# Overlapping image strips in HBM: stored once by line, and cut into strips by the loads

## The chip, the cores and the metric

The kernel runs on one NeuronCore of a Trainium2 chip. Its time is the device time of one execution in microseconds; less is better. Three runs of the kernel before gave a median of 8800.12 us (8797.13 to 8805.94). One further execution was taken by the hardware profiler, and the profile below is of that one.

## What is computed

The input `x` is (4, 64, 256, 256): 4 images, 64 channels, 256 lines of 256 columns, all in float32. Two layers follow one another. The first is a transformer block on images: a layernorm, an attention over channels with a local branch, a residual, a second layernorm and a gated feed-forward pass with depthwise convolutions and a filter of 8 x 8 patches in the frequency domain. The second is a linear attention over rows, one over columns, and an ordinary feed-forward pass. The change touches the gated feed-forward pass of the first layer:

```python
def _mffn(x, in_w, dw3, dw5, out_w, fW):
    t = _conv1x1(x, in_w)                      # 64 -> 256 channels
    x1, x2 = (t[:, :192], t[:, 192:])
    d1 = _dwconv(x1, dw3)                      # 3 x 3, each channel by itself
    x_gate, x1_2 = (d1[:, :128], d1[:, 128:])
    x2 = _dwconv(x2, dw5)                      # 5 x 5, each channel by itself
    y = gelu(x_gate) * concatenate([x1_2, x2], axis=1)
    y = _conv1x1(y, out_w)
    ...                                        # patch filter
```

`t` are the 256 inner channels that the title of the change speaks of; they travel through HBM between two stages of the kernel.

## The kernel before

The program runs in stages, one after another: A (first layernorm, projections, attention statistics), a short rest of the local branch, C1, C2, C3 (output product, patch filter, row attention) and D (column attention and feed-forward pass). Each stage reads what the one before it left in HBM. C1 and C2 matter here.

**C1** walks over 32 blocks of 8 image lines, with two pairs of images in each. For a block it builds the residual stream `xm` (matmuls L775 and L779, DVE L785), transposes and normalizes it (L796, L797, layernorm), turns it back (L810, L812) and multiplies by the feed-forward input weights. That last part is `hidden(s, hf)`: `hf` 0 and 1 stand for the two halves of the 256 inner channels, 128 partitions each. For every two lines, four matmuls (L824, one per image) are copied into a tile `tb` (ACT L830 and DVE L828 in turn) and stored to the HBM tensors `td[0]` or `td[1]` by DMAs that POOL issues: one for `hf` 0 (L842), and two for `hf` 1 (L839, L840), since there the two halves of the column phases change places. A column is 4 t + f, with f its phase and t from 0 to 63; a *line* of one channel and one phase holds 4 images x 64 values of t, which is 1 KB.

**C2** does the depthwise convolutions as banded matmuls, one channel pair (one channel of `td[0]`, one of `td[1]`) per group, 128 groups. The partitions of the operand `t0` or `t1` are the pairs (f, line in strip): 4 phases x 32 lines. An image of 256 lines is covered by NI = 9 strips of 32 lines which begin R0 = 28 lines apart, so neighbouring strips share four lines. The band matrices `w` contract over phases and lines at once (`full`, L882, 128 x 128), and two 64 x 64 parts per tile add what comes from the neighbouring t (`part`, L889). ACT L914 takes the gelu, DVE L915 the product into `y`, and POOL L916 stores `y` to `yd`.

`load(g)` of C2 issues three DMAs on SP's queue: `w` (L872, 192 KB) and `t0`, `t1` (L876, 1152 KB each), into tiles with three buffers. It is called two groups ahead, so the loads of group g + 2 stand in the program before the work of group g and wait for the end of group g - 1, whose buffers they take. The framework that places waits does so from what each instruction reads and writes; nothing else orders the two stages, and the first load of C2 waits for the last store of C1.

In the kernel before, `td` is laid out by strip: `[128 channels, 9 strips, 4 phases, 32 lines, 256]`. A line that lies in two strips is stored twice, by a second DMA from the same `tb`. A strip is then one block of 128 lines of 1 KB, and the load of `t` one DMA for all 128 partitions.

Elsewhere in the program there are loads that reach only some partitions: `xs` of stage A in halves of 64 (L511), `L` of the local branch in quarters of 32 (L445), and `gp` in pieces of 32 and 64 partitions (L592 to L600 in stage A, L745 to L749 in C1).

Of the kernel before, what the change touches and what calls it, by code (L numbers as in the profile page):

```python
# [9 lines left out]
F32 = mybir.dt.float32  # L10
# [4 lines left out]
C, H, W = 64, 256, 256  # L15
# [234 lines left out]
def kernel(ctx: ExitStack, tc: tile.TileContext, x, packs, fd, out, off):  # L250
    nc = tc.nc
    B = x.shape[0]
    V, S, T, G, SY = nc.vector, nc.scalar, nc.tensor, nc.gpsimd, nc.sync
# [3 lines left out]
    dram = ctx.enter_context(tc.tile_pool(name="dram", bufs=1, space=bass.MemoryType.DRAM))  # L257

    def mm():
        return ps.tile([128, 512], F32, tag="mm", name="mm")  # L260
# [22 lines left out]


    NI, R0 = 9, 28
    td = [dram.tile([128, NI, 4, 32, B * W // 4], F32, name=f"td{v}") for v in (0, 1)]
    yd = dram.tile([128, 4, 32, NI, B * W // 4], F32, name="yd")


# [37 lines left out]
    p = sp1.enter_context(tc.tile_pool(name="pst", bufs=2))  # L327
# [386 lines left out]
    def stage_c1():  # L714
        NS = H // 8
        with ExitStack() as cs:
            p = cs.enter_context(tc.tile_pool(name="pc", bufs=2))
# [3 lines left out]
            t = mm()  # L721
# [6 lines left out]
            t = mm()  # L728
# [88 lines left out]
            def hidden(s, hf):  # L817

                for y in range(4):
                    tb = p.tile([128, 8, B, W // 4], F32, name="tb", bufs=5)  # L820
                    for b in range(B):
                        q = slice(b % 2 * 64, b % 2 * 64 + 64)
                        t = mm()
                        T.matmul(t, inT[q, hf * 128:(hf + 1) * 128],  # L824
                                 xls[b // 2, s][q, :, 2 * y:2 * y + 2].rearrange("p f y t -> p f (y t)"), start=True, stop=True)
                        o, i_ = tb[:, :, b, :], t.rearrange("p (f t) -> p f t", f=8)
                        if b % 2:
                            V.tensor_copy(o, i_)  # L828
                        else:
                            S.copy(o, i_)  # L830
                    y0 = 8 * s + 2 * y
                    tf = tb.rearrange("p (f y) b t -> p f (y b t)", f=4)
                    for i in range(NI):
                        r = y0 - R0 * i
                        if 0 <= r < 32:
                            dst = td[hf][:, i, :, r:r + 2].rearrange("g f r e -> g f (r e)")

                            if hf:
                                G.dma_start(dst[:, 2:4], tf[:, 0:2])  # L839
                                G.dma_start(dst[:, 0:2], tf[:, 2:4])  # L840
                            else:
                                G.dma_start(dst, tf)  # L842
                    yield

            def after(*gens):
# [10 lines left out]
            for n in range(len(seq) + 3):  # L856
                if n + 1 < len(seq):
                    load(*seq[n + 1])
                _steps(after(back(*seq[n - 2]) if 1 < n < len(seq) + 2 else None, hidden((n - 3) // 2, (n - 3) % 2) if n > 2 else None),
                       front(*seq[n]) if n < len(seq) else None)  # L860
# [4 lines left out]
    def stage_c2():  # L865
        with ExitStack() as cs:
            p = cs.enter_context(tc.tile_pool(name="pe", bufs=2))
            NW = 192

            def load(g):  # L870
                w = p.tile([128, 2 * NW], F32, name="w", bufs=3)
                SY.dma_start(w, fd[:, 2 * NW * g:2 * NW * (g + 1)])  # L872
                xs = []
                for v in (0, 1):
                    t = p.tile([128, NI * B, W // 4], F32, tag=f"t{v}", name=f"t{v}", bufs=3)
                    SY.dma_start(t.rearrange("p (n b) t -> p n (b t)", b=B), td[v][g].rearrange("n f r e -> (f r) n e"))  # L876
                    xs.append(t)
                ld[g] = w, xs

            def full(t, w, x_, c):  # L880
                n = (c.stop - c.start) * 64
                T.matmul(t[:, :n], w[:, 0:128], x_[:, c, :], start=True, stop=False, skip_group_check=True)  # L882

            def part(t, w, x_, c, dt, turned):

                n = (c.stop - c.start) * 64
                o, i_, po = (slice(0, 63), slice(1, 64), 64) if dt > 0 else (slice(1, 64), slice(0, 63), 0)
                q = 64 - po if not turned else po
                T.matmul(t[po:po + 64, :n].rearrange("p (n c) -> p n c", c=64)[:, :, o], w[q:q + 64, 128:192],  # L889
                         x_[q:q + 64, c, i_], start=False, stop=True, skip_group_check=True)  # L890

            ld = {}
            load(0)
            load(1)
            for g in range(128):
                if g + 2 < 128:
                    load(g + 2)
                w, xs = ld.pop(g)
                y = p.tile([128, NI * B, W // 4], F32, name="y", bufs=3)
                ws = [w[:, v * NW:(v + 1) * NW] for v in (0, 1)]  # L900
                for i in range(0, NI, 4):
                    cs_ = [slice(k * B, min(k + 2, NI) * B) for k in range(i, min(i + 4, NI), 2)]
                    ts = [[mm() for c in cs_] for v in (0, 1)]
                    for v in (0, 1):
                        for t, c in zip(ts[v], cs_):
                            full(t, ws[v], xs[v], c)
                    for k, c in enumerate(cs_):
                        for dt in (1, -1):
                            for v in (0, 1):
                                part(ts[v][k], ws[v], xs[v], c, dt, v)  # L910
                    for k, c in enumerate(cs_):
                        n = (c.stop - c.start) * 64
                        ge = p.tile([128, 512], F32, name="ge", bufs=4)
                        S.activation(ge[:, :n], ts[0][k][:, :n], AF.Gelu)  # L914
                        V.tensor_tensor(y[:, c, :].rearrange("p n c -> p (n c)"), ge[:, :n], ts[1][k][:, :n], ALU.mult)  # L915
                G.dma_start(yd[g].rearrange("f r n e -> (f r) (n e)"), y.rearrange("p n t -> p (n t)"))  # L916
# [496 lines left out]
```

## Time and profile before

| | before |
|---|---|
| three runs: median (lowest to highest) | 8800.12 us (8797.13 to 8805.94) |
| the profiled execution | 8803.6 us |
| its span on the core | 8801.8 us |
| granted TensorE clock, mean | 0.969 |
| HBM read, written | 967.65 MB, 788.53 MB |
| queue q1 (SP's loads), share of 16 engines over the span | 39.0% |
| queue q0 (POOL's stores), share of 16 engines over the span | 28.0% |
| `t<-td` loads, L876 | 256 of 1152 KB, median 9.9 us from issue to landing |
| `td<-tb` stores, L842 | 144 of 1024 KB, median 15.6 us |
| `td<-tb` stores, L839 and L840 | 288 of 512 KB, median 13.9 us |

The profile names an instruction by its line, its engine and the tiles it writes and reads (`t<-td`). PE is the engine of the matmuls, PEld its weight loads, DVE the vector engine, ACT the scalar engine, POOL and SP the two that issue DMAs here. All DMAs run on the same 16 DMA engines, whichever queue they come from. A share of 16 engines is the time that the packets of a queue took, divided by 16 times the length of the stretch. In the rows of 40 slices a digit is the busy share in tenths of one fortieth of the span (220 us). A row of waits reads: who waited, for whom, us in total, times, longest.

### The profile page before, as it was taken

Reading aid. Unit: us, or ns where it says so; the run is one execution under the profiler, and the core shown is the slowest. Engines: PE = TensorE matmul, PEld = TensorE weight load, DVE = VectorE, ACT = ScalarE, POOL = GpSimd, SP = SyncE. Lnnn points to the kernel's source line nnn. Section 1 sums busy time; section 2 is a strip of 40 time slices with the busy share of each in tenths; the row PEclk is TensorE's granted clock in tenths of the full one; section 3 lists DMA queues with packets and bytes.
Section 4 is the critical chain, followed back from the end, with each engine's and each line's share of the span. In section 5 each row is a group of like instructions: output and inputs, shape, how many; then the busy total and the mean of one; then the engine's idle time right before and its main releaser. Section 6 shows DMA issues by size and latency. Waiting matters only on the chain. (4 is left out here: it accounts for less than half of the span.)

```text
span 8801.8 us, 143151 instructions
## 1 busy us (share of the span) xinstructions
PE 8178.1 (93%) x57518; PEld 4216.6 (48%) x57518; DVE 5927.4 (67%) x8506; ACT 4601.7 (52%) x7779; POOL 1205.2 (14%) x1828
## 2 busy tenths in 40 slices
PE   8999999699999998999999999999997999999998
PEld 6777777344444443333333344444443444444443
DVE  7766666377777774222222288888886888888886
ACT  4455455455555553222222266666663777777776
POOL 1111111212222221000000011111110010101011
PEclk9999999699999999999999999999997999999999
DMA  7777777799999998888888755555552232323232
GB/s 161 161 188 187 182 182 180 193 347 388 396 391 388 386 387 320 298 296 298 296 297 298 273 184 172 173 168 167 169 158 63 59 77 58 77 58 77 58 77 39
DMA packets 1258502, 1832.48 MB, mean 208 GB/s; under 512 B 335600, under 2 KB 1040112, under 8 KB 1196656
## 3 DMA queue, kind: packets, MB, share of 16 engines
q1 hardware_dynamic: 1053296, 1034.63, 39.0%
q0 software_dynamic: 204544, 788.69, 28.0%
q8 instruction: 456, 7.47, 0.3%
q14 instruction: 206, 1.69, 0.1%
HBM read 967.65 MB, written 788.53 MB: 200 GB/s over the span
## 5 line engine op out<-in xcount | busy, mean ns | idle before, releaser
L915 DVE TENSOR_TENSOR y<-ge,mm 128x512 f32<-128x512 f32 (+1 forms) x640 | 406.3, 635 | 1212.8 <-ACT ge L914 1212.8
L882 PE MATMUL mm<-t,w 128*128 128x512 f32 (+1 forms) x2560 | 1094.1, 566 | 18.8 <-DMA t<-td 18.8
L914 ACT ACTIVATE ge<-mm 128x512 f32<-128x512 f32 (+1 forms) x640 | 354.9, 555 | 1253.5 <-PE mm L889 1253.5
L775 PE MATMUL mm<-gp,wc 128*64 128x510 f32 (+1 forms) x3072 | 702.7, 596 | 90.8 <-DVE xm L785 51.4
L620 PEld LDWEIGHTS mm<-wqk,gp 128*128 128x128 f32 x6144 | 728.7, 197 | 99.2 <-issue 61.5
L882 PEld LDWEIGHTS mm<-t,w 128*128 128x128 f32 x2560 | 455.4, 190 | 647.5 <-issue 437.0
L620 PE MATMUL mm<-wqk,gp 128*128 128x128 f32 x6144 | 762.3, 282 | 1.1 <-POOL gp L589 0.9
L1341 PE MATMUL mm<-xfT,w 64*128 64x512 f32 x2048 | 620.9, 642 | 51.1 <-ACT hg L1343 26.8
L1343 ACT ACTIVATE hg<-mm,b 128x512 f32<-128x512 f32 x1024 | 634.1, 688 | 53.2 <-PE mm L1341 51.5
L830 ACT COPY tb<-mm 128x512 f32<-128x512 f32 x512 | 300.7, 588 | 632.4 <-PE mm L824 632.1
L889 PE MATMUL mm<-t,w 64*64 64x504 f32 (+1 forms) x5120 | 575.6, 555 | 0.0
L824 PE MATMUL mm<-xl,pack_c 64*128 64x512 f32 x2048 | 513.5, 601 | 8.1 <-ACT xl L812 4.7
L1358 PE MATMUL mm<-hg,pack_d 128*64 128x512 f32 x2048 | 505.8, 615 | 0.0
L775 PEld LDWEIGHTS mm<-gp,wc 128*64 128x64 f32 x3072 | 277.8, 137 | 470.5 <-issue 333.3
L316 ACT ACTIVATE ln_sq<-xn 128x1024 f32<-128x1024 f32 x256 | 274.3, 1072 | 365.4 <-DVE xn L314 365.3
L1365 POOL DMA_DIRECT2D out_dram<-st x128 | 209.1, 1638 | 1756.3 <-DVE fe L695 1543.6
L318 DVE TENSOR_REDUCE ln_v<-ln_sq 128x16 f32<-128x1024 f32 x256 | 312.0, 1219 | 186.0 <-ACT ln_sq L316 186.0
L970 PE MATMUL mm<-ya,pack_e 128*64 128x512 f32 x1024 | 381.2, 616 | 11.2 <-DMA ya<-yd 11.2
L828 DVE COPY tb<-mm 128x512 f32<-128x512 f32 x512 | 345.0, 685 | 24.0 <-PE mm L824 18.5
L1359 DVE TENSOR_SCALAR st<-mm,pack_d 128x512 f32<-128x512 f32 x256 | 281.1, 1098 | 117.9 <-PE mm L1358 117.6
L1341 PEld LDWEIGHTS mm<-xfT,w 64*128 64x128 f32 x2048 | 225.1, 192 | 276.1 <-issue 125.7
L1185 ACT ACTIVATE ln_sq<-xc 128x1024 f32<-128x1024 f32 x256 | 273.0, 1067 | 132.1 <-DVE xc L1183 132.1
(458 smaller groups left out, 15283.8 us busy)
## 6 DMA issues: line engine op xcount, KB each, us to landing
t<-td SPq DMA_DIRECT2D x256, 1152.0 KB, 9.9
td<-tb POOLq DMA_DIRECT2D x144, 1024.0 KB, 15.6
td<-tb POOLq DMA_DIRECT2D x288, 512.0 KB, 13.9
yd<-y POOLq DMA_DIRECT2D x128, 1152.0 KB, 10.1
ya<-yd SPq DMA_DIRECT2D x192, 512.0 KB, 5.7
xs<-in_x_dram SPq DMA_DIRECT2D x128, 512.0 KB, 6.8
projd<-pj POOLq DMA_DIRECT2D x256, 256.0 KB, 6.0
gp<-projd SPq DMA_DIRECT2D x128, 512.0 KB, 9.5
```

Of the source, the lines that this page charges most:

```text
L620: T.matmul(qp[:, k * 128:(k + 1) * 128], gp[:, 2 * i + k // 2, at + dx:at + dx + 128], wqk[:, dx, :], start=(dx == 0), stop=(dx == 2))
L775: T.matmul(tv[i * 64:(i + 1) * 64, :, o], wc[2 * pr + i][:, dx, :], gps[i][:, 2 * r:2 * r + 2, i_], start=(dx == 1), stop=False, skip_grou ...
L824: T.matmul(t, inT[q, hf * 128:(hf + 1) * 128], xls[b // 2, s][q, :, 2 * y:2 * y + 2].rearrange("p f y t -> p f (y t)"), start=True, stop=True)
L828: V.tensor_copy(o, i_)
L882: T.matmul(t[:, :n], w[:, 0:128], x_[:, c, :], start=True, stop=False, skip_group_check=True)
L889: T.matmul(t[po:po + 64, :n].rearrange("p (n c) -> p n c", c=64)[:, :, o], w[q:q + 64, 128:192], x_[q:q + 64, c, i_], start=False, stop=Tr ...
L914: S.activation(ge[:, :n], ts[0][k][:, :n], AF.Gelu)
L915: V.tensor_tensor(y[:, c, :].rearrange("p n c -> p (n c)"), ge[:, :n], ts[1][k][:, :n], ALU.mult)
L970: T.matmul(t[b * 64:(b + 1) * 64, :], owT, ya[:, :, 2 * r:2 * r + 2, b * 64:(b + 1) * 64].rearrange("p f y t -> p y f t"), start=True, sto ...
L1341: T.matmul(t, w1[rh * 64:(rh + 1) * 64, k * 128:(k + 1) * 128], xT[rh * 64:(rh + 1) * 64], start=True, stop=True)
L1343: S.activation(g, t, AF.Gelu, bias=b1[:, k:k + 1])
L1358: T.matmul(y[rh * 64:(rh + 1) * 64, :], w2[:, k, :], hg[k * 2 + rh], start=False, stop=(k == 1), skip_group_check=True)
```

## The change

`td` is laid out by image line: `[128 channels, 4 phases, 260 lines, 256]`, of which lines 0 to 255 are written and read. Each pair of lines is stored once; the loop over strips in `hidden` goes, and with it the second store of shared lines. The strips are cut by the loads: the load of `t0` or `t1` becomes four DMAs, one for each phase f. Each goes to 32 partitions, and reads 32 lines (step 1 KB) of 9 strips (step R0 lines, 28 KB), 1 KB from each. Lines shared by two strips are read twice, as before. The tiles in SBUF, the matmuls and everything else stay.

```diff
-    td = [dram.tile([128, NI, 4, 32, B * W // 4], F32, name=f"td{v}") for v in (0, 1)]
+    td = [dram.tile([128, 4, H + 4, B * W // 4], F32, name=f"td{v}") for v in (0, 1)]
...
                     tf = tb.rearrange("p (f y) b t -> p f (y b t)", f=4)
-                    for i in range(NI):
-                        r = y0 - R0 * i
-                        if 0 <= r < 32:
-                            dst = td[hf][:, i, :, r:r + 2].rearrange("g f r e -> g f (r e)")
-
-                            if hf:
-                                G.dma_start(dst[:, 2:4], tf[:, 0:2])
-                                G.dma_start(dst[:, 0:2], tf[:, 2:4])
-                            else:
-                                G.dma_start(dst, tf)
+                    dst = td[hf][:, :, y0:y0 + 2].rearrange("g f r e -> g f (r e)")
+
+                    if hf:
+                        G.dma_start(dst[:, 2:4], tf[:, 0:2])
+                        G.dma_start(dst[:, 0:2], tf[:, 2:4])
+                    else:
+                        G.dma_start(dst, tf)
...
                     t = p.tile([128, NI * B, W // 4], F32, tag=f"t{v}", name=f"t{v}", bufs=3)
-                    SY.dma_start(t.rearrange("p (n b) t -> p n (b t)", b=B), td[v][g].rearrange("n f r e -> (f r) n e"))
+                    for f in range(4):
+
+                        src = td[v][g, f]
+                        win = bass.AP(tensor=src.tensor, offset=src.offset, ap=[[B * W // 4, 32], [R0 * B * W // 4, NI], [1, B * W // 4]])
+                        SY.dma_start(t[f * 32:f * 32 + 32].rearrange("p (n b) t -> p n (b t)", b=B), win)
                     xs.append(t)
```

## The prediction

> **What bounds the kernel now.** I read the busy line and the 40 slices first, then asked the trace for the stretches of the two stages that the change touches: C1 (about 1720 to 3410 us, it writes `td`) and C2 (3420 to 5042 us, it reads `td`).
>
> ```profile
> PE 8178.1 (93%) x57518; PEld 4216.6 (48%) x57518; DVE 5927.4 (67%) x8506; ACT 4601.7 (52%) x7779; POOL 1205.2 (14%) x1828
> ...
> PE   8999999699999998999999999999997999999998
> ...
> DMA  7777777799999998888888755555552232323232
> GB/s 161 161 188 187 182 182 180 193 347 388 396 391 388 386 387 320 298 296 298 296 297 298 273 184 172 173 168 167 169 158 63 59 77 58 77 58 77 58 77 39
> ```
>
> PE is busy nearly throughout, and two stages also have DMA engines close to full: slices 9 to 15 (C1, some 390 GB/s) and 16 to 22 (C2, some 297 GB/s). In such stages one must ask which of the two sets the pace. For C2, the timeline of PE over one channel group:
>
> ```profile
> 4007.99 3.70 PE L882 MATMUL mm<-t,w 128*128 128x512 f32 x8
> ...
> 4020.02 0.66 PE L889 MATMUL mm<-t,w 64*64 64x252 f32 x8
> 4020.60 0.70 PE L882 MATMUL mm<-t,w 128*128 128x512 f32 x1
> ```
>
> (start, duration, instruction.) One group takes 4020.60 - 4007.99 = 12.61 us, and PE has no gap in it. PE's waits over the stage and the DMA queues of 3500 to 5000 us:
>
> ```profile
> PE mm L882 <- DMA t<-td: 18.8, 1, 18.8
> ```
>
> ```profile
> q1 hardware_dynamic: 294810, 303.84, 64.4%
> q0 software_dynamic: 17138, 140.40, 22.1%
> ```
>
> PE waits for a load once, at the stage's start. The 16 DMA engines are used 64.4 + 22.1 = 86.5%: PE sets the pace, but only 1.7 us of each 12.61 us are free on the DMA engines. That is the whole cover.
>
> For C1 the trace holds an experiment of its own. Some steps store a pair of lines twice (strips overlap), some once. Three equal stretches of two steps each, columns: stretch, length, busy us (count) of PE, PEld, DVE, ACT, POOL, clock, DMA share, GB/s:
>
> ```profile
> 2109.69:2160.99 51.30, 48.67 (x240) 23.59 (x240) 40.83 (x57) 27.82 (x49) 9.80 (x15) 1.00 1.02 375
> 2160.99:2212.53 51.54, 48.92 (x240) 23.65 (x240) 40.74 (x57) 27.81 (x49) 12.88 (x19) 1.00 1.02 395
> 2316.57:2367.90 51.33, 48.68 (x241) 23.60 (x241) 40.66 (x57) 27.86 (x49) 11.45 (x17) 1.00 1.02 393
> ```
>
> The second has four POOL instructions, all DMA issues, more than the first (19 against 15) and is 0.24 us longer; the third has two more and is 0.03 us longer. So the second copies cost C1 nearly nothing, although its DMA engines read as full.
>
> **The change, part by part.**
>
> *Stores (C1).* 144 stores of 1 MB per array become 128: 16 of L842's and 32 of L839/L840's go, 2 x 16 x 1.05 = 33.6 MB. POOL is saved 48 x 0.7 us (0.72 us each in the stretches above) on an engine busy 14%: nothing. PE's gain by the rows above is 0.03 us for two extra issues to 0.24 us for four: 48 issues give 1 to 3 us. PE's waits between 1850 and 3300 us give an upper end for relief: 3.3 us for `gp`. I take -3. The last stores (lines 248 to 255) were stored once already, so the drain that C2's first load waits for stays. The store's pieces stay 2 KB; only its address steps change (1152 to 1040 KB from channel to channel, 32 to 260 KB from f to f). No row shows such a change alone; between 1% of C1's 1630 us lost and as much won (16 us, my estimate: PE covers the rest, as in the three stretches) I take nothing.
>
> *SP's issues (C2).* Two `t` loads per group become eight. L876's median issue is 0.422 us, so SP spends 6 x 0.42 = 2.5 us more per group, beside its waits of 11 us per group for PE (1333.0 us in 123 waits). Hidden. Behind them in SP's queue stand only the next group's loads.
>
> *PE's waits (C2).* The first matmul of a group now depends on nine loads, not three. The trace has semaphore instructions of 51 ns at L882, two per group; six more are 0.3 us per group, 39 us over 128 groups if nothing hides them, 0 if PE waits for data anyway. I take 0; the 39 belongs to the rival below.
>
> *Size and number of packets.* Bytes (2 x 1.18 MB per group) and pieces (1 KB) are unchanged; the new pattern steps 28 KB from strip to strip where the old one stepped 128 KB. No row shows such a step alone: between nothing and the loss that I leave to the slow rival.
>
> *32 partitions per load.* This is the term that matters. Each quarter load writes 32 partitions: f = 0, 1 the lower 64, f = 2, 3 the upper 64. `t` now takes, per group, q1's 64.4% of 1500 us over 119 groups = 8.12 us of all 16 engines, of which `w` has 0.20 of 2.56 MB = 0.62 us, leaving 7.5 us for 2.36 MB: 315 GB/s. How fast are loads that reach only part of the partitions? Stage A loads `xs` as 64 partitions in one half, in 1 KB pieces, with the store queue silent (1054.8 to 1057.2 us):
>
> ```profile
> DMA packets 482, 0.49 MB, mean 203 GB/s; under 512 B 6, under 2 KB 482, under 8 KB 482
> ...
> q1 hardware_dynamic: 482, 0.49, 114.4%
> ```
>
> All engines are busy, and move 203 GB/s. The `L` load is the very shape of the new one, four loads of 32 partitions after one another, but in 8 KB pieces (1648.0 to 1652.4 us):
>
> ```profile
> DMA packets 178, 1.04 MB, mean 236 GB/s; under 512 B 51, under 2 KB 51, under 8 KB 51
> ...
> q1 hardware_dynamic: 178, 1.04, 101.6%
> ```
>
> And a mixed stretch of stage A with 32-partition loads (1012.5 to 1015.5 us) has q1 at 0.41 MB for 71.8% of 3 us = 190 GB/s. So 2.36 MB take 10.0 us (236), 11.6 us (203) or 12.4 us (190). I take 11.6: same piece size, from HBM, queue alone.
>
> Add `w` 0.62 and the `yd` store's 22.1% of 1500/119 = 2.79 us: 15.0 us of DMA per group. Some comes back. In the 203 GB/s stretch all engines are busy and still slow, so they hold each other up on the way to the same half; an engine that is moving a store packet leaves that way to the others. At best, load packets run at today's pace for 2.79 us: 2.79/7.5 of the load instead of 2.79/11.6, a saving of 13% of 11.6 = 1.5 us. But the stores fall together: from 4014.5 to 4018.5 us q0 takes 67.9% of all engines. So a third of it: 0.5 us. **14.5 us per group**, above PE's 12.61. The 1.7 us of cover are used up, and the DMA engines set the pace; what is late next is PE, which waits about 1.9 us per group for `t`, and its semaphores and SP's issues lie under that wait.
>
> The Trainium skill, "SBUF — State Buffer", section "Door 1: The DMA port swizzle (why [64,N] ≈ [32,N])", speaks against the change: 32 neighbouring partitions, and 64 of one half, reach 8 of the 16 ports through which DMAs enter. Of its 435 GB/s half would be left, 217.6, an estimate from that page: 2.36 MB in 10.8 us and a group in 10.8 + 0.62 + 2.79 - 0.5 = 13.7 us. The trace has 203 below it and 236 above it, so the row, not the rule, stands in my sum.
>
> *Sum.* Now C2 takes 128 x 12.61 = 1614 us after its first load. At 14.5 us it is 1856 us: +242. C1 gives -3; the last groups' stores follow the last loads instead of delaying them, -2 x 2.79, and the first load, 4 us longer (11.6 - 7.5), is already in the 128. Together +233 on the profiled execution's 8803.6 us (span 8801.8): 9037. The median shown is 8800.1, 3.5 us under that execution; I give **9035**.
>
> **Rivals.** A difference under 0.2% (18 us) can't be told from none here.
> 1. *Hidden.* The quarters of neighbouring loads fall on opposite halves and overlap, as `L` at 236 GB/s suggests: 10.0 + 3.41 less at best 0.9 (2.79/7.5 - 2.79/10.0 of 10.0) = 12.5 us, just under 12.61. Then C2 keeps its time: 4 us for the first load, -3 for C1, 0 to 39 for semaphores: 8801 to 8840. For: `L`'s shape. Against: its 8 KB pieces; the 1 KB rows are 203 and 190. 0.11.
> 2. *Faster.* C1's DMA share of 1.02 is the true bound and the removed stores come off it: 33.6 MB at 390 GB/s = 86 us, to 8715, if C2 stays at 12.61. It decides from 18 us on, that is when a fifth of the 86 shows and C2 loses nothing. Against it: 51.54 beside 51.30 us. 0.04.
> 3. *Worse.* Engines in lockstep, 190 GB/s, no relief: 15.8 us per group, +408 - 9 = 9200; if the 28 KB steps read slower than any 1 KB row here, say 17 us, 9350. For: the lowest row. 0.13 for above 15.8.
> 4. *Forecast.* 13.0 to 15.8 us per group. 0.72.
>
> **How the numbers follow.** The likeliest case gives 9035. The range runs from 8845 (about 13.0 us per group) to 9225 (just past 15.8): it holds the forecast and the lower part of rival 3, leaving out rivals 1 and 2 and the upper part of 3, about 0.2. Faster: 0.04, and 0.01 of rival 1 (C1 gains more than 3), 0.05. Same: 0.06 of rival 1. Slower: 0.04 of rival 1 (its semaphores), 0.13 and 0.72, 0.89.
>
> **What would show it.** Right: after the change, PE's waits name `t` in nearly every group, some 2 us each; q1's packet time rises from 52 ns (64.4% of 16 x 1500 us over 294810 packets) to about 80; the DMA share of C2 reads 1.0 and GB/s drops to about 260; C1's step stays at 51.3 us for two. Wrong: C2's group still 12.61 us, or C1's step shorter, or `t` packets at 52 ns beside a longer group, which would put the cause on issue or waits, not on the partitions.

## The result and the profile after

| | before | after |
|---|---|---|
| runs on this chip: median (lowest to highest) | 8798.62 us (8796.94 to 8805.94), 4 runs | 9056.96 us (9052.23 to 9066.99), 4 runs |
| the profiled execution | 8803.6 us | 9054.15 us |
| its span | 8801.8 us | 9052.4 us |
| granted TensorE clock, mean | 0.969 | 0.972 |

The changed kernel takes 1.0296 times as long, 95% interval 1.0283 to 1.0308. The forecast of 9035 us lies 22 us from it. **The cause that the forecast gave is nevertheless not the cause.** It said that PE would stand still for 1.9 us per group and wait for `t`. PE does not wait.

The page of after, busy line and slices (a slice is now 226 us):

```profile
PE 8422.2 (93%) x57518; PEld 4260.4 (47%) x57518; DVE 5922.0 (65%) x8506; ACT 4600.6 (51%) x7779; POOL 1165.6 (13%) x1780
...
PE   8999999699999999999999989999997899999998
...
DMA  7777777799999989999999975555553223232332
GB/s 164 161 188 179 184 188 170 232 362 368 369 368 369 368 332 267 255 257 254 256 256 258 253 208 169 170 170 168 169 171 98 54 59 75 57 75 60 71 70 43
```

C2 is now slices 15 to 22 (counted from 0), with the DMA engines at 9 and some 256 GB/s: just what the forecast wanted to see. But the first line contradicts it. PE has the same 57518 matmuls as before and is *busy* for 8422.2 us instead of 8178.1, 244.1 us more. A wait for data makes idle time, not busy time. The waits of PE in C2, and the DMA queues of 3500 to 5200 us:

```profile
PE mm L883 <- DMA t<-td: 22.1, 1, 22.1
```

```profile
q1 hardware_dynamic: 299868, 297.58, 78.3%
q0 software_dynamic: 16832, 137.88, 22.0%
```

One wait of 22.1 us at the stage's start, where before had one of 18.8, and none in the 127 groups that follow. The DMA engines read 100.3% used beside a PE that never lacks data. A hundred microseconds in the middle of the stage (length, busy us (count) of PE, PEld, DVE, ACT, POOL, clock, DMA share, GB/s) say the same in one line:

```profile
4300.00:4400.00 100.00, 100.00 (x415) 35.12 (x411) 21.79 (x35) 19.41 (x35) 3.20 (x6) 1.00 1.00 255
```

PE is busy 100.00 of 100.00 us at full clock. Where the time goes is seen in the timeline of PE over one group of after (start, duration, instruction, count):

```profile
4209.24 1.98 PE L883 MATMUL mm<-t,w 128*128 128x512 f32 x4
4211.15 1.91 PE L890 MATMUL mm<-t,w 64*64 64x504 f32 x8
4212.99 1.98 PE L883 MATMUL mm<-t,w 128*128 128x512 f32 x4
4214.90 1.91 PE L890 MATMUL mm<-t,w 64*64 64x504 f32 x8
4216.74 3.70 PE L883 MATMUL mm<-t,w 128*128 128x512 f32 x8
4220.37 1.92 PE L890 MATMUL mm<-t,w 64*64 64x504 f32 x16
4222.22 1.13 PE L883 MATMUL mm<-t,w 128*128 128x256 f32 x4
4223.28 0.66 PE L890 MATMUL mm<-t,w 64*64 64x252 f32 x8
4223.87 1.55 PE L883 MATMUL mm<-t,w 128*128 128x512 f32 x3
```

A group takes 4223.87 - 4209.24 = 14.63 us, and every group from the second on takes exactly that. Before, the group that the prediction shows goes on after its first line (3.70 us, x8, from 4007.99) so:

```profile
4011.62 1.92 PE L889 MATMUL mm<-t,w 64*64 64x504 f32 x16
4013.47 3.70 PE L882 MATMUL mm<-t,w 128*128 128x512 f32 x8
4017.10 1.92 PE L889 MATMUL mm<-t,w 64*64 64x504 f32 x16
```

The source text of these matmuls is the same in both kernels, their order is not. Each matmul of the source shows as two instructions. Before, the first four tiles of a group run as 8 instructions of `full` (`t0`, then `t1`) and then 16 of the 64 x 64 parts, those of `t0` and `t1` in turn. After, everything of `t0` comes first (4, then 8), then everything of `t1` (4, then 8). The framework chose this order when it scheduled the program. And look at the durations: **8 instructions of the parts, by tensor, take 1.91 us, as long as 16 in turn, 1.92 us.** How many of them run at once is seen in the first 0.4 us of such a row, of after and of before:

```profile
4211.15 0.64 PE L890 MATMUL mm<-t,w 64*64 64x504 f32 x2
```

```profile
4011.62 0.65 PE L889 MATMUL mm<-t,w 64*64 64x504 f32 x4
```

By tensor two of them start together (7 ns apart) and the next two 0.42 to 0.47 us later; in turn four start together (within 20 ns), and the next four after the same time. So four run at once in turn, and only two by tensor; what lies behind that is tested with e8 and e11. The second four tiles still run as before (x8, x16). One tensor's share of the four tiles takes 4212.99 - 4209.24 = 3.75 us, before it was half of 4013.47 - 4007.99, 2.74 us. Twice the difference is 2.02 us, and 14.63 - 12.61 = 2.02. Over 128 groups that is 259 us.

The whole difference of the two spans, 250.6 us, splits so: from the first to the last group's start in C2 1603.6 us before, 1860.3 after, +256.7; the way to the first group of C2 is 8.7 us shorter; what follows the last group's start is 2.6 us longer.

### The profile page after: what moved, and what is told of

It reads as the page before. It is cut to its first block, busy times and chain, and to the rows that moved or that the text cites. A ratio compares the mean times of both kernels' runs of the same rounds, so it can differ in the third digit from the quotient of the medians.

```text
span 9052.4 us, 144108 instructions
## 1 busy us (share of the span) xinstructions
PE 8422.2 (93%) x57518; PEld 4260.4 (47%) x57518; DVE 5922.0 (65%) x8506; ACT 4600.6 (51%) x7779; POOL 1165.6 (13%) x1780
## 5 line engine op out<-in xcount | busy, mean ns | idle before, releaser
L883 PE MATMUL mm<-t,w 128*128 128x512 f32 (+1 forms) x2560 | 1128.0, 571 | 22.1 <-DMA t<-td 22.1
L890 PE MATMUL mm<-t,w 64*64 64x504 f32 (+1 forms) x5120 | 818.3, 556 | 0.0
L775 PE MATMUL mm<-gp,wc 128*64 128x510 f32 (+1 forms) x3072 | 701.5, 595 | 89.9 <-DVE xm L785 51.9
L775 PEld LDWEIGHTS mm<-gp,wc 128*64 128x64 f32 x3072 | 278.0, 137 | 468.1 <-issue 329.2
L890 PEld LDWEIGHTS mm<-t,w 64*64 64x64 f32 x5120 | 213.7, 132 | 548.2 <-issue 548.2
```

Of the source, the lines that this page charges most:

```text
L775: T.matmul(tv[i * 64:(i + 1) * 64, :, o], wc[2 * pr + i][:, dx, :], gps[i][:, 2 * r:2 * r + 2, i_], start=(dx == 1), stop=False, skip_grou ...
```

## The experiments

Two theories were set against each other. **Load theory** (the forecast): quarter loads reach half of the partitions at a time, are slower, and PE waits for them. **Order theory**: the quarter loads only make the framework give PE another order; its own matmuls then take 2.02 us longer per group. A group's time below is from one start of the group's first matmul to the next.

### e1: the change, with PE's order held as written

```diff
-            for g in range(128):
+            with tc.manual_schedule(engines={mybir.EngineType.PE}):
+                for g in range(128):
...
```

> The kernel after, with PE's order in C2 held as the program is written (the 64x64 matmuls of t0 and t1 in turn). Order theory (the quarter loads made the scheduler put all of t0's matmuls ahead of t1's in the first four tiles of each group, which costs PE 2.02 us per group): the group leaves 14.63 us. It falls to 12.61 if the loads keep up (about 8790 us in all, C1's 9 us gained), or to the pace of the DMA engines, which I put at 13.6 to 14.0 us from the gap of nearly 1 us in which the load queue is idle at the end of each group of the kernel after (8920 to 8980 us). Load theory (the prediction: 32-partition loads take 14.5 us per group, PE waits for them): the order changes nothing, the group stays at 14.5 to 14.6 us and the time at 9040 to 9060.

Measured: 8820.44 us (10 runs; before on the same chip 8801.99), ratio 1.0022, 1.0013 to 1.0031. Of the 2.96% that the change costs, 0.22% remain. The stores and loads are those of after; only PE's order is that of before. PE's timeline near the start of the stage, and its waits:

```profile
3448.26 1.98 PE L883 MATMUL mm<-t,w 128*128 128x512 f32 x4
3450.63 1.96 PE L883 MATMUL mm<-t,w 128*128 128x512 f32 x4 [0.39 <-DMA t<-td]
3452.52 1.92 PE L890 MATMUL mm<-t,w 64*64 64x504 f32 x16
```

```profile
PE mm L883 <- DMA t<-td: 34.3, 16, 22.5
```

Again 16 parts in 1.92 us. Now there are waits for `t`, in brackets: the second half of the first eight matmul instructions reads `t1`, which has just not landed. Groups 2 to 11 take 12.61 to 14.36 us, nearly all later ones 12.61. So the load theory has a true part of some 17 us (C2 from the first to the last group's start 1621.0 us against 1603.6): 1 us in group 1, (13.45 - 12.61) x 10 = 8 us in groups 2 to 11, and as much in ten later groups. The order theory had put 8790 us for loads that keep up and 8920 to 8980 for loads that do not; e1 lies between.

### e2: the kernel before, with the order of after

Loads and stores of before; PE held, and in the first four tiles the work is done tensor by tensor.

```diff
+            with tc.manual_schedule(engines={mybir.EngineType.PE}):
...
-                    for v in (0, 1):
+                        for vs in (((0,), (1,)) if i == 0 else ((0, 1),)):
+                            for v in vs:
...
-                            for v in (0, 1):
+                                    for v in vs:
...
```

> The kernel before, loads and stores untouched, with PE's order of the kernel after in the first four tiles of each group (t0's, then t1's). Order theory: 14.63 us per group, C2 longer by 128 x 2.02 = 259 us, 9055 to 9060 us. Load theory: the 128-partition loads still take 11 us of DMA per group, nothing changes: 12.61 us and 8800.

Measured: 9053.32 us, ratio 1.0284, 1.0269 to 1.0299; 14.63 us per group. PE's timeline of e2:

```profile
4215.59 1.98 PE L882 MATMUL mm<-t,w 128*128 128x512 f32 x4
4217.51 1.91 PE L889 MATMUL mm<-t,w 64*64 64x504 f32 x8
4219.35 1.98 PE L882 MATMUL mm<-t,w 128*128 128x512 f32 x4
4221.26 1.91 PE L889 MATMUL mm<-t,w 64*64 64x504 f32 x8
```

Line for line the group of after, from loads of 128 partitions. The order alone gives the whole loss. With e1 that settles it: the order is sufficient (e2), and without it nearly nothing is left (e1). Holding PE's order costs nothing by itself: e11 below is before with its own order held, and takes 12.61 us per group.

### e3: before's layout and stores, with loads in quarters, order left to the framework

```diff
-                    SY.dma_start(t.rearrange("p (n b) t -> p n (b t)", b=B), td[v][g].rearrange("n f r e -> (f r) n e"))
+                    for f in range(4):
+                        SY.dma_start(t[f * 32:f * 32 + 32].rearrange("p (n b) t -> p n (b t)", b=B), td[v][g][:, f].rearrange("n r e -> r n e"))
```

> The kernel before with the quarter loads alone: td still laid out by strip and shared lines stored twice, PE's order left to the scheduler. Both theories: C2 as in the kernel after (14.5 to 14.6 us per group). What it tells apart is the stores: if storing once is worth the 9 us by which C2 started earlier after the change, this is 9 us slower than the kernel after (about 9066); if that was chance, the same 9057. Should the group come out longer than 14.63, reading by line is faster than by strip.

Measured: 9055.34 us, ratio 1.0286, 1.0269 to 1.0303; 14.63 us per group, and one wait for `t` (22.2 us). Loads in quarters are all it takes for the framework to change the order; the layout by line and its 28 KB steps are not needed for it. Storing shared lines twice or once cannot be told apart in the medians (9055.3 here, 9057.0 in after, not timed beside one another). Why the framework decides so was not tried and stays open.

### e4 and e5: how fast the loads are by themselves

To see the pace of the transfers, PE was made so quick that it must wait for them: its order held, and the 64 x 64 parts of C2 left out. e4 does this to after, e5 to before.

```diff
...
-                    for k, c in enumerate(cs_):
-                        for dt in (1, -1):
-                            for v in (0, 1):
-                                part(ts[v][k], ws[v], xs[v], c, dt, v)
...
```

> The kernel after with the 64x64 matmuls of C2 left out (what comes from the neighbouring t is not added), PE's order held as written. PE then needs 3.70 + 3.70 + 1.13 = 8.5 us per group, and the pace of C2 is that of the DMA engines with quarter loads. Load theory: 14.5 us per group. Order theory, by the idle gap: 13.6 to 14.0. If it is under 12.61, the loads would have been hidden and the whole loss is PE's order.

> The kernel before (128-partition loads) with the 64x64 matmuls of C2 left out (what comes from the neighbouring t is not added), PE's order held as written: the reference for e4, whose groups took 13.4 to 13.7 us at the start of C2 and 12.0 on average. The prediction's accounts give 10.95 us of DMA per group for these loads (86.8% of 12.61), PE 8.5. So 10.9 to 11.0 us, the same from the first groups to the last. If it also starts slow and then falls, the slow start is not a matter of the quarters.

Measured (one execution each): e4 8714.9 us, e5 8408.83 us. PE's waits in C2 of e4, and of e5:

```profile
PE mm L883 <- DMA t<-td: 363.8, 177, 22.2
```

```profile
PE mm L882 <- DMA t<-td: 178.1, 131, 19.9
```

With 177 and 131 waits in 128 groups, a group's time is near the transfers' pace (an upper bound: PE has work of its own between the waits). Loads of 128 partitions: 9.59 us per group on average, where 10.9 to 11.0 were expected. Loads in quarters: 12.00 on average, 13.42 in groups 2 to 11 and 11.87 after them. So quarter loads are slower, by 12.00 - 9.59 = 2.4 us per group; but on average they end before PE's 12.61, and the cover that before has is 12.61 - 9.59 = 3.0 us and not 1.7.

### e6, e7, e10: what makes the remaining waits of e1 go

e6 is e1 with the loads of f = 2 and 3 on ACT's queue instead of SP's, e7 is e1 with the four loads in the order 0, 2, 1, 3, so that neighbours in the queue go to opposite halves of the partitions; e10 is e7 once more, with more runs.

```diff
-                        SY.dma_start(t[f * 32:f * 32 + 32].rearrange("p (n b) t -> p n (b t)", b=B), win)
+                        (SY if f < 2 else S).dma_start(t[f * 32:f * 32 + 32].rearrange("p (n b) t -> p n (b t)", b=B), win)
```

```diff
-                    for f in range(4):
+                    for f in (0, 2, 1, 3):
```

> e1 (the kernel after with PE's order held) with the quarter loads f = 2, 3 issued from ACT's queue instead of SP's, so that loads to the lower and the upper 64 partitions stand in two queues at once. If loads are slow because neighbouring ones go to the same half (the account of the prediction), the slow first ten groups of e1 (13.0 to 14.4 us) go: 12.61 throughout, some 12 us less than e1, 8790 in the profile and at or under the kernel before (8795 to 8805 in the median). If the quarters are slow for being small, groups stay at 13 to 14 and the time at e1's 8820 or above it, as ACT then issues eight DMAs more per two groups.

> e1 with the quarter loads in the order f = 0, 2, 1, 3: one queue, but neighbouring loads go to different halves of the partitions. If engines that run a load apart (18 packets of 1 KB each) relieve each other, half the lead suffices here: fewer slow groups at the start than e1's ten, 8800 to 8815. If only two queues help: ten or more slow groups, 8820.

> e7 again with more rounds, since its interval (0.9983 to 1.0001) left open whether it beats the kernel before. Its C2 started 11 us earlier than in the profile of the kernel before and lost 3 us in its first group: if that gain is real, 0.9992 again, 5 to 9 us under the kernel before; if not, 1.000.

Measured against before on the same chip: e6 8800.18 us, 0.9999 (0.9990 to 1.0008); e7 8792.27 us, 0.9992 (0.9983 to 1.0001); e10 8800.86 us, 0.9998 (0.9989 to 1.0007). The slow groups of e1 are gone: e6 has two (23.03 and 14.34 us), e7 one (15.51), and from then on every group takes 12.61 us. e7's interval ends at 1.0001 and e10 does not repeat its 0.08%, so the version with the order held and the loads alternating is as fast as before; that it is faster is not shown. It is about 2.9% faster than the change as it was made.

The queues of e6, and of e7 (both 3500 to 5000 us), hold a small surprise:

```profile
q1 hardware_dynamic: 161783, 163.76, 37.1%
q10 hardware_dynamic: 144687, 140.39, 30.5%
```

```profile
q1 hardware_dynamic: 307093, 304.80, 82.4%
```

In e6, 67.6% of 16 x 1500 us over 306470 packets is 53 ns per packet, and before had 52. In e7, with the order 0, 2, 1, 3 in one queue, it is 64 ns; in e1, with 0, 1, 2, 3, 66 (83.3% of 16 x 1400 us over 285047, 3600 to 5000 us); PE sets about the same pace in all four. So from two queues that serve opposite halves, quarter loads take no more of the DMA engines' time than whole ones, and alternating in one queue hardly lowers it. After has 71 ns (78.3% of 16 x 1700 us over 299868), at 14.63 us per group: the same loads as in e1, with more time, show longer packets. How fast the loads of e6 are by themselves was not tried.

### e9: alternating loads, transfers by themselves

e4 with the order 0, 2, 1, 3.

> e4 (C2 without its 64x64 matmuls, so that what comes from the neighbouring t is not added) with the quarter loads in the order 0, 2, 1, 3 of e7: the pace of the loads by themselves. e4 took 13.4 to 13.7 us in its first groups and 12.0 on average, 128-partition loads (e5) 9.6. If e7's order takes away the slow start, as its steady 12.61 suggests: under 12.6 in the first groups and 10.5 to 11.5 on average. If e7 was only lucky in how the engines fell: like e4.

Measured: 8685.44 us (one execution); 11.78 us per group on average, over the 10.5 to 11.5 that were expected; 12.54 in groups 2 to 11, and very uneven (8.16 to 16.39). Alternating helps the first groups (13.42 in e4), hardly the later ones (11.71 against 11.87).

### e8 and e11: which 64 x 64 matmuls run at once

A `part` reads 64 partitions (rows of the array) and writes 64 partitions of a tile in PSUM, where matmuls put their results (columns of the array). It so takes a quarter of the array. By the code of `part`, the two parts of a tile of `t0` lie on a diagonal: lower rows with upper columns, and upper rows with lower columns. Those of `t1` lie on the other diagonal. In turn, four neighbours therefore cover all four quarters; by tensor, neighbours only ever cover the two of one diagonal, and add to the same PSUM tile. e8 is e2 with the parts of a tensor in another order, so that neighbours write different PSUM tiles; they stay on the diagonal. e11 is before, with PE held, in which all parts read `t0`; order and quarters stay.

```diff
+                                for k, dt in ((0, 1), (1, -1), (0, -1), (1, 1)):
+                                    part(ts[v][k], ws[v], xs[v], cs_[k], dt, v)
...
```

```diff
-                                part(ts[v][k], ws[v], xs[v], c, dt, v)
+                                    part(ts[v][k], ws[v], xs[0], c, dt, v)
...
```

> e2 with the four 64x64 matmuls of t0 (and of t1) in another order: first tile's from the lower rows, second tile's from the upper rows, first tile's upper, second tile's lower. Neighbours then use different rows of the array, different columns of it and different PSUM banks. In e2 neighbours into one bank didn't overlap, in the kernel before those of t0 and t1 (different rows, same columns, different banks) did. If the bank is what parts them, two of three neighbours overlap now: 12.61 us per group. If the columns are: 14.63, as in e2.

> The kernel before, PE's order as it is, but the 64x64 matmuls of t1's tiles read their moving data from t0 too (wrong values for the second array). Neighbours still use different rows and the same columns of the array and different PSUM banks; but as in e2 and e8 they now read one tile. If it is the columns that let neighbours overlap: 12.61 us per group, 8800. If it is that they read two tiles: all pairs are lost, ten of them against e2's four with 2.02 us, that is 12.61 + 2.02 x 2 + 0.5 = some 17 us per group and 9370.

Measured (one execution each): e8 9060.04 us, 14.63 us per group; e11 8802.24 us, 12.61 us per group. The parts in the first four tiles of a group (for e8, those of one tensor) as a whole and in their first 0.4 us, in e8 and then in e11:

```profile
4217.43 1.91 PE L889 MATMUL mm<-t,w 64*64 64x504 f32 x8
...
4217.43 0.64 PE L889 MATMUL mm<-t,w 64*64 64x504 f32 x2
```

```profile
4011.51 1.92 PE L889 MATMUL mm<-t,w 64*64 64x504 f32 x16
...
4011.51 0.65 PE L889 MATMUL mm<-t,w 64*64 64x504 f32 x4
```

Both expectations took it that neighbours on a diagonal do not overlap and that pairs with the same columns do. The starts say otherwise: two at once in e8, as in after and e2; four at once in e11, as in before. That the two which start together belong to two matmuls, and are not the two instructions of one, is seen in the semaphore updates by which PE reports a finished tile. In e8 the third matmul ends the first tile and the fourth the second, and the updates stand on the seventh and eighth of the eight instructions, 7 ns apart. Were the matmuls issued one after the other, the third's would stand on the sixth; in e4, where `full` ends a tile, every second instruction has one.

So other PSUM tiles do not bring back the pace (e8), and one source tile does not take it away (e11). Neither changes the quarters, and these decide: two matmuls on the two quarters of a diagonal take as long as four on all four, and by tensor half of the array stands idle. Pairs in the same rows or the same columns alone were not tried.

The Trainium skill, "TensorEngine Tiling (Array Packing)", section "Key Properties", says that different tiles of the array can load weights and multiply in parallel. The runs agree: two at once on a diagonal (8 instructions in 1.91 us), four at once on all four quarters (16 in 1.92 us).

## Why the prediction came out near, for the wrong reason

**The step that failed** is "14.5 us per group, above PE's 12.61 ... the DMA engines set the pace; what is late next is PE, which waits about 1.9 us per group for `t`". The transfers needed 12.0 us per group (e4), less than 12.61; PE's own work grew to 14.63. That both come to about 14.5 is chance. The forecast took it that with the matmuls their time stays too, and had no term for the order in which the framework would issue them. None of the four rivals held it either. Point by point:

- *What bounds C2 before* (PE at 12.61 us): right. e5 shows that the transfers alone would do with 9.59 at most.
- *Cover of 1.7 us per group*: too small; it is at least 3.0. The busy share of 86.5% was read as if each packet's time were fixed. e5 moves the same loads and stores in 9.59 us, where 86.5% of 12.61 would be 10.9.
- *Quarters, 11.6 instead of 7.5 us* (+4.1, less 0.5 of relief): mis-sized on average. The pace rose by 2.4 us (12.00 - 9.59) over the stage; in groups 2 to 11 by 4.1 (13.42 - 9.28), there as worked out. The row that was chosen is a lone load of 2.5 us, and it answers to the start of the stage. The pace then fell within the same run, for the same loads.
- *The estimate from the Trainium skill*, "SBUF — State Buffer", section "Door 1: The DMA port swizzle (why [64,N] ≈ [32,N])": its 13.7 us per group are near groups 2 to 11 of e4 (13.4) and above e4's mean of 12.0. Its rate for half the ports, 217.6 GB/s, is not contradicted: e4 loads 2.36 MB of `t` per 12.0 us, 197 GB/s on average. Too long is the sum that puts `w` and the store after the loads; e4 moves 314 GB/s in all (3500 to 4900 us), so they ran beside them.
- *Stores, -3 us*: C1 gains somewhat more. From the first L775 to the first group of C2 seven profiles with single stores have a mean of 1683.5 us, six with double stores 1690.0: -6.5 (1682.4 to 1685.1 against 1686.7 to 1691.8). In before some steps of C1 are longer than the usual 25.6 us (up to 27.9); in after none passes 25.94, the first few left aside. That is far from rival 2's 86 us: C1's DMA share went from 1.01 to 0.99 and its GB/s from 385 to 367 (1800 to 3300 us), at nearly the same time per step.
- *The last stores, -2 x 2.79 us*: not seen. What follows the last group's start is 2.6 us longer in after.
- *SP's issues and semaphores at nothing*: right. e7 has nine loads per group and 12.61 us, as before with three.
- *28 KB steps at nothing*: e3 (128 KB steps) and after (28 KB) have the same 14.63 us, but PE covers the loads in both, so this bounds them only.
- *Rival 1* (hidden) comes nearest to what the loads do by themselves: e1 at 8820 lies in its 8801 to 8840.
- *The signs*. DMA share 1.0 (1.00), 260 GB/s (257), C1's step 51.3 us for two (51.3) came true, packet time 80 ns (71) in part. They were no proof, for a PE that is slower for its own reasons leaves the same traces, and transfers that have time are stretched into it. Waits of PE for `t` in nearly every group were the only sign that could tell the two apart, and it failed: one wait, 22.1 us.

That the DMA pace falls within C2 because the 16 engines come out of step with one another, so that some serve one half of the partitions while others serve the other, would fit e6, e7 and e9; it is argued and not shown.

## What to carry to other kernels

Where a framework orders the instructions, an edit to the loads can reorder an engine whose code it does not touch: compare the order of that engine in both traces before any cost is put down to the transfer. A period that is the same to a hundredth of a microsecond in every group, with more busy time for as many instructions, is an engine's own work and not a wait for data; and DMA engines that read 100% used prove no bound while nobody waits for them. Where small matmuls share the array, issue those that cover different quarters as neighbours, and hold that order by hand.

## What the runs showed of the hardware that was not expected

- Float32 matmuls of 64 x 64 run at once when their neighbours cover different quarters of the array: four on four quarters (16 instructions in 1.92 us), two on a diagonal (8 in 1.91 us). Two on a diagonal that add to one PSUM tile (after) take as long as two that write different tiles (e8).
- The same loads moved at 13.42 us per group in groups 2 to 11 of e4 and at 11.87 in the rest.
- Loads that reach 32 partitions each took 66 ns per packet from one queue in the order 0, 1, 2, 3 (e1), 64 in the order 0, 2, 1, 3 (e7), and 53 from two queues that serve opposite halves (e6). In e6 and e7, and in nearly all groups of e1, PE and not the loads set the pace, so these are no limits.
- The DMA share reads 1.07 in e4 (4300 to 4400 us) at 325 GB/s and 1.00 in after at 255 GB/s: the share says little of what the engines could still move.
